# Green's 60 comparators for blocks of 16 rows, in place of the odd-even merges' 63, in the sort of a quantile kernel

## The chip, the core and the metric

The kernel runs on one core of a Trainium2 chip. Its engines are TensorE (PE, matmuls), VectorE (DVE, elementwise), ScalarE (ACT, here mostly copies), GpSimd (POOL, here the issuer of indirect DMAs) and SyncE (SP, plain DMAs). They run side by side and wait for each other by semaphores. The metric is device time in microseconds, the median of several runs.

## What is computed

Two graph layers over 4096 nodes of 128 features. The first is an attention layer with 8 heads over the neighbours that the 4096 x 4096 matrix `adj` names. The second takes, for every node and every feature, three quantiles of the neighbours' values; only it matters here:

```python
keep = mask & ~remove                  # each node's neighbours, some removed
n_keep = keep.sum(axis=1)
vals = jnp.where(keep[:, :, None], x[None, :, :], big)
svals = jnp.sort(vals, axis=1)
for q in (0.25, 0.5, 0.75):
    idx = jnp.maximum(jnp.ceil(q * n_keep).astype(jnp.int32) - 1, 0)
    picked = jnp.take_along_axis(svals, idx[:, None, None], axis=1)[:, 0, :]
    agg = agg + w_q * picked
```

The mean of the three is mixed half and half with the node's own value, goes through a 128 x 128 linear layer, and `x` is added.

## The kernel before

The first part (lines 160 to 1430) finds the neighbours of every node and computes the attention layer; it fills roughly the first 4000 us. A branch on a flag then chooses between `general`, a dense path that isn't taken with these inputs, and `sparse` (line 1699), the sort.

**Tiles.** `sparse` works through 32 tiles of 128 nodes, one node in each partition. The nodes are ordered by their number of neighbours, so that tile t needs at most `HIGH[t]` rows: 50 for tile 0, rising to 80 for tile 30 and 100 for tile 31. `load` (line 1884) gathers a tile's rows with one indirect DMA of POOL for each row (line 1726): a row is one neighbour's 128 float32 features in every partition, 128x128 elements. The tile `rows` has three buffers, and tile t+1 is loaded ahead of the phase of tile t. Missing neighbours are filled with very large and very small values.

**The network.** The rows are put in order by a sorting network: fixed pairs (a, b) of rows, of which the smaller goes to a and the larger to b, for all nodes and features at once. `swap_layers(w)` (line 1501) gives the pairs for w rows in layers: Batcher's odd-even merges, with n the power of two from w upwards. `comparators(n)` (line 1441) yields the pairs of numbers (p, k) with p = 1, 2, 4, ..., n/2, and for each p, k = p, p/2, ..., 1. The layers with p below 16 sort each block of 16 rows, in 10 layers and 63 comparators; those with p = 16 and p = 32 merge the blocks. `needed_swaps` (line 1513) drops the comparators, or single outputs of one, that no wanted rank depends on. A tile with 66 to 80 rows sorts 64 of them in this way and the others apart (`plan`, line 1682), and `quantile` (line 1779) joins the two lists for the ranks that may be picked.

**Steps.** `steps` (line 1578) makes instructions of a layer's comparators: those with the same distance b - a whose lower rows form a regular pattern (runs in a grid of up to two strides, `rectangles`, line 1540) are one step, cut (`pieces`, line 1561) to at most `PAIRS` = 16 comparators. `compare` (line 1751) emits a step. Where both outputs are needed, ACT copies the lower rows aside (line 1764), and DVE takes the minimum of copy and upper rows into the lower rows and the maximum into the upper ones (line 1771). The copy is in one of two PSUM buffers named `low` if it has more than `SMALL` = 4 rows, else in one of four buffers named `low_s`. Steps with one needed output are one DVE instruction without a copy (lines 1775 and 1777).

**Order.** `plan` cuts a tile's layers in two: `second` is the last merge (6 layers for 64 rows), `first` all before it. In phase t, `interleave` (line 1612) mixes `second` of tile t-1 and `first` of tile t: from the steps whose predecessors are done it always takes the one that DVE can begin soonest by a small count of costs. Behind the list, `quantile` and `pick` of tile t-1 are added; the pieces of `pick` and `finish` (ACT's scaling of the picked rows at line 1826, PE's sums at 1833 and 1861, ACT's copies at 1843 and 1869) stand in the list `waiting` and are emitted one at a time between later steps, the PE pieces only beside a step of 5 to 12 rows. The framework that assigns semaphores may still move single instructions a little, such as a maximum behind the next step's minimum.

Of the kernel before, what the change touches and what calls it, by code (L numbers as in the profile page):

```python
# [1440 lines left out]
def comparators(n):  # L1441

    p = 1
    while p < n:
        k = p
        while k:
            yield p, k
            k //= 2
        p *= 2
# [48 lines left out]
    return a  # L1498


def swap_layers(w):

    n = 1 << (w - 1).bit_length()
    for p, k in comparators(n):
        yield [
            (i + j, i + j + k)
            for j in range(k % p, n - k, 2 * k)
            for i in range(k)
            if (i + j) // (2 * p) == (i + j + k) // (2 * p) and i + j + k < w
        ]  # L1510
# [171 lines left out]
def plan(t):  # L1682

    wide = HIGH[t]
    extra = wide - MAIN if MAIN < wide <= 80 else 0
    w = wide - extra
    needed = {i - 1 for lo, hi in places(t) for i in range(lo - extra, hi + 1)}
    layers = needed_swaps(swap_layers(w), needed)
    merge = (w - 1).bit_length()

    first = steps(layers[:-merge], lambda i: i, PAIRS if t else PAIRS // 4)
    second = steps(layers[-merge:], lambda i: i)
    if extra:
        apart = needed_swaps(swap_layers(extra), range(extra))
        first += steps(apart, lambda i: MAIN + extra - 1 - i)
    return first, second, extra
# [650 lines left out]
```

## Time and profile before

| | |
|---|---|
| median of 3 timed runs | 8359.05 us (8342.91 to 8362.36) |
| span of the profiled execution | 8384.6 us |
| attention layer and neighbour search | to about 4000 us |
| quantile sort | from about 4000 us to the end |
| two-output comparisons on DVE (line 1771) | 2768 instructions, 4044.6 us busy |
| copies for them on ACT (line 1764) | 1384 instructions, 1708.2 us busy |
| gathers of rows on POOL (line 1726) | 2078 instructions, 2031.9 us busy |

The profile is of one execution, taken by the hardware profiler. Its span runs from the first to the last instruction. A page gives busy time and idle time by engine, and groups of instructions by source line, with the shapes of output and inputs; "128x2048" is 128 partitions by 16 rows of 128 features. "idle before" is time in which the engine stood still just ahead of the group, with what released it. A timeline gives start, length, engine, line and operation, in microseconds.

### The profile page before, as it was taken

What the parts mean: (1) busy time and instruction counts of PE and PEld (TensorE: products, weight loads), DVE (VectorE), ACT (ScalarE), POOL (GpSimd) and SP (SyncE); (2) the same over time, 40 slices, a digit from 0 to 9 for tenths busy, and PEclk for the clock granted to TensorE, in tenths of its full rate; (3) what the DMA queues carried; (4) which work ended last, traced back from release to release, by engine and by line L of the source; (5) the groups of instructions that cost most, each with busy time, mean ns of one, the idle gap of its engine ahead of it and who ended that gap; (6) DMA issues with size and microseconds to landing.
All of it is one profiled execution on the core that took longest, in us unless ns stands there. A gap on an engine that the chain in (4) does not pass through costs nothing. (4 is left out here: it accounts for less than half of the span.)

```text
span 8384.6 us, 31455 instructions
## 1 busy us (share of the span) xinstructions
PE 1235.7 (15%) x6047; PEld 1032.2 (12%) x6047; DVE 5886.7 (70%) x9454; ACT 2218.9 (26%) x2338; POOL 4358.1 (52%) x4524
## 2 busy tenths in 40 slices
PE   2122222222332332330000000000000000000000
PEld 1121212222231322230000000000000000000000
DVE  6454564454222222224899999999999999999899
ACT  5021121000000000002344443443443433333333
POOL 3545546656666666666455456445554545354410
PEclk5565656565565666565555555555555555555555
DMA  6122222112112111111011111111111111011100
GB/s 192 43 89 71 74 77 64 49 38 50 50 48 50 50 49 50 50 41 39 26 36 35 33 36 43 31 32 38 34 34 31 38 30 35 27 34 32 31 9 1
DMA packets 219060, 380.98 MB, mean 45 GB/s; under 512 B 129283, under 2 KB 129412, under 8 KB 218852
## 3 DMA queue, kind: packets, MB, share of 16 engines
q0 software_dynamic: 145808, 308.58, 13.9%
q1 hardware_dynamic: 72898, 70.23, 2.8%
q14 instruction: 159, 1.30, 0.1%
q8 instruction: 49, 0.80, 0.0%
q10 hardware_dynamic: 146, 0.07, 0.0%
HBM read 368.26 MB, written 10.31 MB: 45 GB/s over the span
## 5 line engine op out<-in xcount | busy, mean ns | idle before, releaser
L1771 DVE TENSOR_TENSOR rows<-low,rows 128x2048 f32<-128x2048 f32 (+10 forms) x1970 | 3649.3, 1893 | 88.0 <-ACT low L1764 61.7
L1726 POOL DMA_INDIRECT rows<-x_d,info x2078 | 2031.9, 978 | 1863.7 <-ACT picked L1826 1184.2
L975 POOL DMA_INDIRECT nb<-xf_d,ids x2190 | 2078.1, 949 | 1329.5 <-issue 625.3
L1764 ACT COPY low<-rows 128x2048 f32<-128x2048 f32 (+8 forms) x985 | 1528.4, 1557 | 2331.8 <-DVE rows L1771 1665.3
L1115 PE MATMUL ps_z<-spread,nb 128*128 128x128 f32 x4500 | 757.9, 325 | 1491.4 <-issue 737.3
L1107 DVE TENSOR_TENSOR spread<-e,ps_small 128x1152 f32<-128x1152 f32 (+4 forms) x312 | 342.2, 1109 | 804.1 <-remote 594.0
L1115 PEld LDWEIGHTS ps_z<-spread,nb 128*128 128x128 f32 x4500 | 702.4, 237 | 1565.9 <-issue 996.7
L1833 PE MATMUL low<-sixth_i,picked 128*128 128x128 f32 x300 | 74.3, 430 | 4347.7 <-ACT low L1764 3413.6
L1833 PEld LDWEIGHTS low<-sixth_i,picked 128*128 128x128 f32 x300 | 65.0, 322 | 4357.0 <-ACT low L1764 3420.9
L1771 DVE TENSOR_TENSOR rows<-low_s,rows 128x512 f32<-128x512 f32 (+3 forms) x798 | 395.3, 523 | 128.7 <-remote 39.9
L1077 ACT ACTIVATE ps_e<-e 128x256 f32<-128x256 f32 (+4 forms) x64 | 26.1, 408 | 1513.9 <-DVE e L1067 556.2
L190 DVE MAX8 k<-key 128x8 f32<-128x256 f32 x416 | 169.0, 416 | 169.6 <-remote 119.5
L1764 ACT COPY low_s<-rows 128x512 f32<-128x512 f32 (+3 forms) x399 | 179.8, 486 | 281.6 <-DVE rows L1771 172.0
L1873 POOL DMA_INDIRECT out<-o,info x32 | 34.9, 1091 | 397.2 <-ACT o L1869 369.3
L1130 ACT COPY zT<-ps_z 128x512 f32<-128x512 f32 x64 | 37.6, 587 | 742.7 <-remote 586.0
L382 ACT ACTIVATE nz<-a_i 128x1024 bf16<-128x1024 int32 x128 | 134.2, 1049 | 328.9 <-remote 198.6
L190 DVE MAX8 lists<-cand 128x8 f32<-128x176 f32 x416 | 128.1, 332 | 69.7 <-remote 47.1
L192 DVE MATCH_REPLACE8 key<-k,key 128x256 f32<-128x256 f32 x384 | 156.1, 408 | 0.0
L1058 DVE TENSOR_TENSOR e<-nb,ps_small 128x64 f32<-128x64 f32 (+9 forms) x200 | 45.2, 237 | 154.4 <-DMA nb<-xf_d,ids 129.9
L1438 DVE SCALAR_TENSOR_TENSOR zT<-zT,ps_h 128x512 f32<-128x512 f32 x64 | 42.0, 682 | 158.0 <-ACT zT L1437 109.7
L1146 PE MATMUL ps_h<-zT,w_ga 128*128 128x256 f32 x256 | 105.3, 569 | 271.3 <-DVE s L1438 157.2
L1775 DVE TENSOR_TENSOR rows<-rows 128x256 f32<-128x256 f32 (+8 forms) x245 | 142.5, 583 | 1.6 <-DVE rows L1771 1.4
(245 smaller groups left out, 2429.0 us busy)
## 6 DMA issues: line engine op xcount, KB each, us to landing
a_i<-in_adj SPq DMA_DIRECT2D x128, 512.0 KB
nb<-xf_d,ids POOLq DMA_INDIRECT x2190
rows<-x_d,info POOLq DMA_INDIRECT x2078
xf_d<-xf POOLq DMA_DIRECT2D x4, 576.0 KB
xf<-in_x POOLq DMA_DIRECT2D x4, 512.0 KB
meta_d<-rowdata_k SPq DMA_DIRECT2D x4, 324.0 KB
abc_ta<-in_L_gnn_a POOLq DMA_DIRECT2D x2, 512.0 KB
w_ga<-in_L_gnn_W POOLq DMA_DIRECT2D x2, 512.0 KB
```

What stands on the lines that cost most here:

```text
L190: nc.vector.max(out=top, in_=work)
L192: nc.vector.match_replace(out=work, in_to_replace=top, in_values=work, imm_value=gone)
L382: nc.scalar.activation(nz[:, j, :], a_i, AF.Relu, scale=-1.0, accum_out=self.negative[:, k : k + 1],)
L975: gather = nc.gpsimd.indirect_dma_start(out=rows[:, used + i, :], out_offset=None, in_=xf_d, in_offset=bass.IndirectOffsetOnAxis(ap=ids[:, ...
L1107: last = nc.vector.tensor_tensor(spread[:, :m], e[:, at : at + m, :].unsqueeze(2).to_broadcast(shape), own.unsqueeze(1).unsqueeze(3).to_br ...
L1115: product = nc.tensor.matmul(ps_z[:, g, :], rows[:, k, :D], spread[:, i].rearrange("p j h -> p (j h)"), start=i0 + i == 0, stop=i0 + i == ...
L1146: nc.tensor.matmul(ps_h[:, k, :], w_sb[:, h0 + k, :], zT[:, h0 + k, :], start=True, stop=True)
L1726: return nc.gpsimd.indirect_dma_start(out=row, out_offset=None, in_=x1_d, in_offset=bass.IndirectOffsetOnAxis(ap=info[:, col : col + 1], a ...
L1764: nc.scalar.copy(packed, lows)
L1771: done = nc.vector.tensor_tensor(to, packed, highs, op=op)
L1775: nc.vector.tensor_tensor(lows, lows, highs, op=ALU.min)
L1833: product = nc.tensor.matmul(made["ps"], v, to, start=i == 0, stop=i == len(found))
```

## The change

The layers with p below 16 are replaced by a fixed list of ten layers, `SIXTEEN`, applied to every block of 16 rows. Its first four layers compare rows at distances 1, 2, 4 and 8; six irregular layers with 28 comparators follow, so that a block has 60 comparators in place of 63, in as many layers. It is used where the number of rows is 0 or 14 modulo 16 (16, 62, 64 here); at other widths, and for the merges with p = 16 and 32, nothing is changed. In a block cut short by w, comparators that reach beyond w are left out.

```diff
+SIXTEEN = [[(i, i + k) for i in range(16) if not i & k] for k in (1, 2, 4, 8)] + [
+    [(1, 2), (3, 12), (4, 8), (5, 10), (6, 9), (7, 11), (13, 14)],
+    [(1, 4), (2, 8), (7, 13), (11, 14)],
+    [(2, 4), (3, 8), (5, 6), (7, 12), (9, 10), (11, 13)],
+    [(3, 5), (6, 8), (7, 9), (10, 12)],
+    [(3, 4), (5, 6), (7, 8), (9, 10), (11, 12)],
+    [(6, 7), (8, 9)],
+]
+
+
 def swap_layers(w):
 
     n = 1 << (w - 1).bit_length()
+    whole = w % 16 in (0, 14)
+    for layer in SIXTEEN if whole else []:
+        yield [(i + a, i + b) for i in range(0, n, 16) for a, b in layer if i + b < w]
     for p, k in comparators(n):
+        if whole and p < 16:
+            continue
         yield [
             (i + j, i + j + k)
             for j in range(k % p, n - k, 2 * k)
```

## The prediction

> **What bounds the kernel now.** I read the page's busy times and its forty slices first, then the windows of the sorting stage, then the groups by form, then what VectorE waited for, and last single instructions in the timeline.
>
> ```profile
> PE 1235.7 (15%) x6047; PEld 1032.2 (12%) x6047; DVE 5886.7 (70%) x9454; ACT 2218.9 (26%) x2338; POOL 4358.1 (52%) x4524
> ...
> DVE  6454564454222222224899999999999999999899
> ACT  5021121000000000002344443443443433333333
> POOL 3545546656666666666455456445554545354410
> ```
>
> The 70% of DVE is an average over two halves. From slice 20 on, which is from about 4000 us, its digit is 8 or 9 and nobody else's is above 6. That half is the quantile sort, the only code the change reaches. The windows of that half give the share more exactly (columns: window, its length, then busy us and number of instructions of PE, PEld, DVE, ACT, POOL):
>
> ```profile
> 5500.00:6000.00 500.00, 17.87 (x64) 14.60 (x64) 493.00 (x308) 200.22 (x151) 266.32 (x267) 0.50 0.12 35
> 6000.00:6500.00 500.00, 17.45 (x62) 14.18 (x62) 492.31 (x350) 201.18 (x163) 244.15 (x249) 0.50 0.12 33
> 6500.00:7000.00 500.00, 17.45 (x62) 14.18 (x62) 495.82 (x439) 200.97 (x190) 258.72 (x258) 0.50 0.12 34
> ```
>
> DVE works 98.5 to 99.2% of these windows, ACT 40%, POOL about 51%. So a microsecond of DVE work taken out here is a microsecond of the span, as long as DVE stays that full. What it waits for between 5300 and 8000 us, in the table of waits (total us, times, longest):
>
> ```profile
> DVE rows L1771 <- ACT low L1764: 50.0, 18, 22.5
> DVE rows L1771 <- issue: 5.2, 10, 1.6
> ```
>
> Of the 50.0 us, 22.5 and another 14.1 are two single waits (at 7773 and 7127 us) in which the ACT copy in question stood behind the copy of an output from PSUM (L1869), itself late. The other 16 are 13.4 us together, some 0.8 us each.
>
> **The price of one comparison step.** A step with both outputs is an ACT copy of the k lower rows (L1764) and a minimum and a maximum on DVE (L1771), each over 128k elements. From the groups by form (mean ns is the figure before the second bar) and the timeline of DVE:
>
> ```profile
> L1771 DVE TENSOR_TENSOR rows<-low,rows 128x2048 f32<-128x2048 f32 x910 | 2052.7, 2282 | 20.9 <-ACT low L1764 12.0 <-issue 3.2 <-DVE rows L1771 0.5
> L1764 ACT COPY low<-rows 128x2048 f32<-128x2048 f32 x455 | 848.8, 1869 | 1256.0 <-DVE rows L1771 900.6 <-issue 343.4 <-DMA rows<-x_d,info 8.3
> L1771 DVE TENSOR_TENSOR rows<-low,rows 128x1024 f32<-128x1024 f32 x334 | 405.3, 1219 | 30.8 <-ACT low L1764 22.5 <-issue 1.6 <-DVE rows L1771 0.8
> ...
> L1764 ACT COPY low<-rows 128x1024 f32<-128x1024 f32 x167 | 169.6, 1016 | 366.7 <-DVE rows L1771 220.9 <-issue 144.0 <-DVE rows L1777 1.7
> ```
>
> ```profile
> 6118.35 2.28 DVE L1771 TENSOR_TENSOR rows<-low,rows 128x2048 f32<-128x2048 f32 x1
> 6120.54 0.68 DVE L1771 TENSOR_TENSOR rows<-low_s,rows 128x512 f32<-128x512 f32 x1
> 6121.14 1.22 DVE L1771 TENSOR_TENSOR rows<-low,rows 128x1024 f32<-128x1024 f32 x1
> 6122.28 0.68 DVE L1771 TENSOR_TENSOR rows<-low_s,rows 128x512 f32<-128x512 f32 x1
> 6122.88 1.22 DVE L1771 TENSOR_TENSOR rows<-low,rows 128x1024 f32<-128x1024 f32 x1
> ```
>
> The recorded lengths overlap. After the 2048 the next starts 2.19 us later, not 2.28; after the 512, 0.60 (not 0.68); after the 1024, 1.14 (not 1.22). A 512 and a 2048 differ by 1.60 us for 1536 elements, 1.042 ns each, so an instruction takes **0.067 us plus 0.133 us for each row** of 128 elements from start to start.
>
> **The sum.** The plan of each tile can be counted from the code before and after. Widths that are 0 or 14 modulo 16 occur in 20 of the 32 tiles; the merge of the last six layers (`second`) is the same in all.
> - 16 tiles sort 64 rows (HIGH 64 to 76): 5 more steps, so 10 more DVE instructions, and 12 fewer comparators (3 in each of 4 blocks), so 24 fewer row operations: 0.67 - 3.20 = -2.53 us each, -40.5.
> - 3 tiles of 62 rows: 14 more instructions, 22 fewer row operations: -1.99 us each, -6.0.
> - tile 30 (64 rows and 16 apart): 24 more, 30 fewer: -2.4.
>
> Together 226 more instructions (+15.1) and 480 fewer row operations (-64.0): **-48.9 us** of DVE. What changes is the mix: of the steps with both outputs, 111 with 16 rows go and 154 with 8 rows come, 42 with 4, 20 with 12 and some small ones; 1112 steps become 1225. ACT gets 113 copies more, but shorter ones: -111 x 1.87 + 154 x 1.02 and the rest come to -6 us, on an engine that is idle 60% of the stage.
>
> Here a rule speaks against the change. The Trainium skill's "VectorE: DVE Perf Modes" gives a fp32 tensor_tensor (N+151)/0.96 ns (section on the TRN2 errata; it advises tiles of 512 elements and more) and says that the next instruction does not start until the pipeline is empty (section "The DRAIN you can't avoid"). Its length agrees with the rows: (512+151)/0.96 = 691 ns against 684. But as the price of an instruction it would be 0.157 us for each of the 226, +35.5, and leave only -28.5. The starts above say 0.067. The rows of this trace decide; the rule's sum is kept as a rival.
>
> **Dependent neighbours.** Where an instruction needs what the one straight ahead of it on DVE did, the overlap is lost:
>
> ```profile
> 6009.70 6.88 DVE L1771 TENSOR_TENSOR rows<-low,rows 128x2048 f32<-128x2048 f32 x3
> ```
>
> Three free 2048s would take 2.20 + 2.20 + 2.28 = 6.68; here the third takes rows that the second wrote, and 0.20 is lost. A maximum straight behind its own minimum loses 0.13 in the same way (starts 6014.29 and 6016.61 against 2.20). In the order in which the built programs issue on DVE, neighbours of the first kind fall from 128 to 88 and of the second from 165 to 137, because layers of four blocks have two to five steps that are independent of each other, which the greedy list can lay between. 40 x 0.2 + 28 x 0.13 = **-11 us**. From both sides: none of it (the waits only move elsewhere) or all of it; I take all, since it is the issue order itself that is counted.
>
> **Waits for the copy.** A new layer such as (1,4),(2,8),(7,13),(11,14) is two steps of 8 rows, and the next layer's copies need both. A copy of 8 rows is 1.02 us, and the other step's pair beside it is 2 x 1.13, so one independent step covers it; where there is none, the merge steps of the tile before lie between. Bounds: all 16 short waits go (-13), or each of the 20 changed phases gets one more of 1.60, such as the one at 5623.99 us (+32). The copy is nearer to covered (ACT idles 60%), so I take 0.
>
> **What else it touches.** All other instructions are the same and in the same order outside this stage; POOL's gathers are as many (2078 rows). Three row buffers let tile t+1 be gathered during phase t: a gather is issued every 1.25 us, so 66 rows need 83 us of a phase of 124 to 164 us, and a phase shorter by 2.5 us is still covered. The exception is tile 31, with 100 rows: its gathers run from 7875.3 to 8002.4 us, and DVE waits for them at the end of tile 30's phase (2.7 us at 8002). So tile 30's 2.4 us are lost there: +2.4. After that only tile 31 is left (100 rows, unchanged), and its chain ends the program.
>
> Sum: -48.9 - 11 + 2.4 = -57.5. It is made in an execution of span 8384.6; the median of the three timed runs is 8359.05, 25.5 below, while the two long waits above are 36.6 of that span. The sum is of work and does not hang on them. Carried to the median: 8359 - 57.5 = **8301.5 us**, 0.7% faster.
>
> **The rivals.**
> - **Copies come late (slower).** Every added step leaves DVE waiting for its copy. For it: the steps get smaller, and chains of dependent layers are where the waits of today lie. Price: a whole 8-row copy bare, 1.02 us, on 113 steps is +115: 8417. It decides from 0.51 us an added step (57.5 / 113), and is a measurable loss from 0.73. Against: ACT at 40%, two jobs interleaved, and fewer dependent neighbours in the issue order.
> - **The full length counts.** If DVE empties its pipe behind each added instruction, the sum is -28.5 + 2.4: 8333, just at the edge. Against: the starts shown.
> - **Nothing reaches the end.** Gathers or the release of row buffers set the pace of a phase, as for tile 31, and the saved DVE time turns into waiting: 8359. For it: POOL waits 1184 us for row buffers in the page's groups (L1726 behind L1826), so buffers are the limit of gathering. Against: this waiting is POOL's slack; DVE's waits for rows are the one at 8002 us and the first tiles'.
> - **The network isn't one that sorts, or the widths don't occur.** Counted from the plans above, 20 tiles change; a later half of the blocks cut at 62 keeps only comparators below 62, and the rows missing are the largest. I give it nothing.
>
> **Numbers.** As summed 0.76, copies late 0.07, full length 0.09, nothing reaches the end 0.08. A change within 0.3% (25 us) can't be told from none here: the three runs before differ by 19 us. Below: -57.5 - 13 and a run low by 10 gives 8278. Above: the full length's 8333 with a run high by 6: 8339. Range 8276 to 8339. Faster takes the first case and most of the second, 0.84; same 0.10; slower 0.06, the late copies.
>
> **What would show it.** In the profile after: the 128x2048 group of L1771's successor falls by 222, the 128x1024 group grows by 308; DVE's instructions grow by 226, and its busy time, in which overlaps count once (2052.7 / 910 = 2.256), falls by about 50 us. DVE's total wait for ACT copies between 5300 and 8000 should stay near 13 us beside any single long wait. Wrong would be: starts behind 8-row instructions more than 1.14 us apart without a wait (the pipe price), or a wait for ACT at each new layer.

## The result, and the profile after

| | kernel before | changed kernel |
|---|---|---|
| median, 9 runs each, in one session | 8349.96 us (8342.91 to 8362.47) | 8375.19 us (8366.08 to 8382.18) |
| span of the profiled execution | 8384.6 us | 8373.4 us |

The ratio is 1.0025, with a 95% interval of 1.0017 to 1.0034. The changed kernel is slower by 25 us; 58 us less were forecast. (The two profiled spans have the opposite order: that execution of the kernel before was a long one, and entered the sort at 3825.6 us. A second profile of it entered at 3792.5 us, with a span of 8350.8. So the sort is compared below by its own length. In the changed kernel it is longer by 15 to 16 us; the rest of the 25 us lies ahead of it, in code that is the same in both and took 3792.5 to 3825.6 us in three profiled executions.)

The work did shrink as counted. From the page of the changed kernel, busy time by engine and the slices of DVE and ACT:

```profile
PE 1241.1 (15%) x6047; PEld 1038.0 (12%) x6047; DVE 5839.2 (70%) x9680; ACT 2213.3 (26%) x2451; POOL 4353.9 (52%) x4524
...
DVE  6554565463222222224899999999999998997999
ACT  5021121000000000002344444444433343342433
```

DVE has 226 more instructions and is busy 47.5 us less (5886.7 before); ACT has 113 more and is busy 5.6 us less. The groups by form, mean ns of one ahead of the second bar:

```profile
L1786 DVE TENSOR_TENSOR rows<-low,rows 128x2048 f32<-128x2048 f32 x688 | 1546.1, 2280 | 62.8 <-ACT low L1779 51.7 <-issue 8.3
L1786 DVE TENSOR_TENSOR rows<-low,rows 128x1024 f32<-128x1024 f32 x642 | 761.2, 1216 | 36.9 <-issue 29.8 <-ACT low L1779 3.2
```

222 of the 16-row instructions went and 308 of 8 rows came. What did not stay is DVE's share. The same windows as before and two later ones (window, length, busy us and instructions of PE, PEld, DVE, ACT, POOL):

```profile
5500.00:6000.00 500.00, 17.86 (x64) 14.60 (x64) 497.92 (x360) 206.42 (x176) 256.07 (x264) 0.50 0.13 35
6000.00:6500.00 500.00, 17.45 (x62) 14.18 (x62) 479.59 (x381) 198.19 (x178) 267.02 (x277) 0.50 0.14 36
6500.00:7000.00 500.00, 7.08 (x28) 6.19 (x28) 495.95 (x486) 200.74 (x208) 217.11 (x226) 0.50 0.11 30
7000.00:7500.00 500.00, 15.36 (x54) 12.39 (x54) 466.96 (x457) 189.42 (x195) 246.27 (x247) 0.50 0.12 32
7500.00:8000.00 500.00, 15.79 (x56) 12.82 (x56) 428.03 (x398) 175.19 (x181) 224.82 (x233) 0.50 0.13 31
```

Of the kernel before, the prediction showed the first three of these windows, with 98.5 to 99.2%. The other two were less full already (96.8 and 94.2%), and there stand its two long waits:

```profile
7000.00:7500.00 500.00, 15.37 (x54) 12.40 (x54) 484.15 (x436) 194.00 (x181) 223.46 (x227) 0.50 0.11 30
7500.00:8000.00 500.00, 15.80 (x56) 12.82 (x56) 470.96 (x383) 191.57 (x173) 249.54 (x259) 0.50 0.13 34
```

In the changed kernel DVE is full between the stalls (99.6% in the first window), but three windows lack 20 to 72 us each. DVE's waits between 5300 and 8000 us, which were 50.0 us and at most 22.5 before:

```profile
DVE rows L1786 <- ACT low L1779: 74.1, 10, 48.6
DVE rows L1786 <- issue: 44.1, 12, 29.6
DVE rows L1786 <- remote: 9.8, 4, 3.1
```

Every gap of the sort can be added up from the starts of DVE's instructions: from one start to the next, less 0.066 us and 1.042 ns for each element. That price comes from the starts that the prediction showed; a gap is what is left over.

| us | before | changed | difference |
|---|---|---|---|
| instructions at that price | 4279.1 | 4230.0 | -49.1 |
| gaps under 0.1 us | 5.3 | 8.6 | +3.3 |
| gaps of 0.1 to 0.3 us (dependent neighbours) | 44.3 | 33.9 | -10.4 |
| gaps of 0.3 to 3 us | 139.1 | 136.5 | -2.6 |
| gaps over 3 us | 72.3 (9) | 146.2 (14) | +73.9 |
| sort, first to last start | 4539.2 | 4554.3 | +15.1 |

So the gain is there, and a few long waits took more than it brought. The longest, in the timelines of PE, ACT and DVE of the changed kernel (start, length, engine, line, operation; in brackets the idle time before and its releaser):

```profile
7692.71 0.80 PE L1876 MATMUL low<-xs,idf 128*128 128x128 f32 x2 [15.73 <-ACT low L1779]
...
7699.78 0.80 PE L1876 MATMUL low<-lwT,comT 128*128 128x128 f32 x2
```
```profile
7693.41 1.87 ACT L1779 COPY low<-rows 128x2048 f32<-128x2048 f32 x1 [0.76 <-issue]
7747.39 0.58 ACT L1884 COPY o<-low 128x512 f32<-128x512 f32 x1 [52.11 <-remote]
7748.01 3.67 ACT L1779 COPY low<-rows 128x2048 f32<-128x2048 f32 x2
```
```profile
7686.70 14.66 DVE L1786 TENSOR_TENSOR rows<-low,rows 128x2048 f32<-128x2048 f32 x7
7749.91 6.69 DVE L1786 TENSOR_TENSOR rows<-low,rows 128x2048 f32<-128x2048 f32 x3 [48.55 <-ACT low L1779]
```

At the end of each group of four tiles PE does the linear layer: 12 matmuls, 24 passes in the trace (two each), recorded as over by 7700.6. The copy of their result (L1884) starts only at 7747.39. The comparison copy behind it in ACT's queue waits with it, and DVE waits for that one. In the kernel before, ACT at the same place:

```profile
7766.48 0.61 ACT L1764 COPY low_s<-rows 128x512 f32<-128x512 f32 x1
7793.66 0.58 ACT L1869 COPY o<-low 128x512 f32<-128x512 f32 x1 [26.56 <-remote]
```

The page names DVE's wait after the comparison copy and ACT's as "remote", a releaser that it does not resolve; it is found by the semaphore events: the semaphore that PE raises after a matmul moves at 7704.0, 7726.4, 7737.6 and last at 7747.37, 0.02 us before the copy. At the end of group 1, where no row gather runs, it moves 0.01 us after the last matmul (4546.54 and 4546.53). Here 37 row gathers were issued between 7692 and 7739, one each 1.25 us.

So the wait was there before too, 26.6 us of ACT and 22.5 of DVE here and 14.1 at one more group end, and 22.5 and 13.9 in the second profile: it is no accident of one execution. What the change moved is when the matmuls come. The pieces in `waiting` are taken one for each two-output step, and PE's only beside steps of 5 to 12 rows. By the plans, the list `first` of a 64-row tile has 35 such steps instead of 30, and 15 instead of 6 of 8 to 12 rows; the whole phase of the longest wait has 61 instead of 56, and 23 instead of 14 of 5 to 12 rows. So `waiting` is worked off sooner: in that phase the last sums' copy comes 44 us after the first row gather was issued (7682.3 against 7638.3), and 82 us before the change (7763.4 against 7681.4). The gathers take 100 us in both. The matmuls that stood near their end now stand in their middle. How late the copy came after the last matmul, at the ends of groups 5, 6 and 7: 1.3, 14.6, 21.0 us before; 15.9, 27.7, 46.8 after. In all six cases the copy starts 9 to 13 us after the phase's last row gather was issued (10.0, 10.0 and 13.1 us before; 9.7, 11.2 and 9.3 after): what comes late in these phases is released shortly behind the end of the gathers.

### The profile page after: what moved, and what is told of

Same layout as the page of the kernel before. It is cut to its first block, busy times and chain, and to the rows that moved or that the text cites. A ratio compares the mean times of both kernels' runs of the same rounds, so it can differ in the third digit from the quotient of the medians.

```text
span 8373.4 us, 31685 instructions
## 1 busy us (share of the span) xinstructions
PE 1241.1 (15%) x6047; PEld 1038.0 (12%) x6047; DVE 5839.2 (70%) x9680; ACT 2213.3 (26%) x2451; POOL 4353.9 (52%) x4524
## 5 line engine op out<-in xcount | busy, mean ns | idle before, releaser
L1786 DVE TENSOR_TENSOR rows<-low,rows 128x1024 f32<-128x1024 f32 (+8 forms) x2076 | 3527.5, 1745 | 139.5 <-ACT low L1779 84.7
L1779 ACT COPY low<-rows 128x2048 f32<-128x2048 f32 (+9 forms) x1038 | 1488.8, 1440 | 2141.8 <-DVE rows L1786 1619.5
L1786 DVE TENSOR_TENSOR rows<-low_s,rows 128x512 f32<-128x512 f32 (+3 forms) x918 | 462.2, 534 | 143.2 <-remote 45.3
L1779 ACT COPY low_s<-rows 128x512 f32<-128x512 f32 (+3 forms) x459 | 211.4, 496 | 402.2 <-DVE rows L1786 254.8
L1130 ACT COPY zT<-ps_z 128x512 f32<-128x512 f32 x64 | 37.6, 588 | 775.1 <-remote 628.0
```

The costliest lines, as they stand in the source:

```text
L1779: nc.scalar.copy(packed, lows)
L1786: done = nc.vector.tensor_tensor(to, packed, highs, op=op)
```

## The experiments

The theory after the first look: PE's output matmuls complete late while row gathers run, and that hides the network's gain. Rivals: the network's shorter steps cost more by themselves; or those matmuls are slow whatever runs. The runs are from four chips. On three of them the kernel before takes 8350 to 8382 us; the fourth, called the faster chip below, is another case, to which a paragraph of its own comes back. Unless said otherwise a ratio is against the kernel before on the same chip, with its 95% interval. "Late" is the copy's start after the recorded end of the last matmul, at groups 5, 6, 7.

**Moving the matmuls in time.** First a second look at the kernel before (8352.57 us), then three kernels in which only the moment of the output changes.

> The kernel before, unchanged, for a profile of an ordinary execution: the profile at hand spans 8384.6 us, 35 us over the median of the timed runs. If the two long waits in it (14.1 and 22.5 us, behind output sums of TensorE that completed late) come and go from run to run, this one shows less of them: span near 8348 with long waits of 0 to 25 us. If they are always there, the span is near 8385 again and the median was something else.

Eighteen empty entries in the list ahead of the output, in the changed kernel:

```diff
-            return [("bank", layer), ("copy", layer_copy)]
+            return [*[("copy", lambda: None)] * 18, ("bank", layer), ("copy", layer_copy)]
```

> The changed kernel, but the four output sums of a group of tiles are issued 18 steps (about 45 us) later, when the row gathers of that phase are over. Theory A (the gain of the network, some 57 us, is there, but the sums now fall into the middle of the gathers, TensorE's completions come 16 to 47 us late there, the copy of their result stands in ACT's queue ahead of the comparison copies, and DVE waits): the four long waits, some 95 us, go, and the time falls from 8375 to 8280-8305. Theory B (the shorter steps themselves cost more than the rows say): nothing of the network changes here, so the time stays within 10 us of 8375.

8448.33 us, 1.0114 (1.0099 to 1.013). Eight such entries in the kernel before:

> The kernel before with the output sums 8 steps (about 26 us) later, which takes them past the end of the gathers there. Theory A: what long waits it ordinarily has (0 to 37 us) go: 8315 to 8350. Theory B: unchanged, 8350.

8511.83 us, 1.0185 (1.0171 to 1.0199). Both forecasts failed, and in the same way. (Group 7, for which they were meant, did come sooner, 8.8 and 12.5 us late.) The entries that were meant to carry the late groups past the gathers carried the early ones into the next phase's. Groups 1 to 5 of the first are now 8 to 34 us late and groups 1 to 4 of the second 30 to 33, where groups 1 to 4 had been on time in both (0.04 us); groups 5 and 6 of the second came on time. Then the other way, the output earlier in the kernel before, its network untouched:

```diff
-APART = 22
+APART = 12
```

> The kernel before, its network untouched, with the sums of the picked rows 12 steps behind their scaling instead of 22, so that they and the output sums fall some 33 us earlier, into the middle of the gathers, as in the changed kernel. Theory A: it gets the changed kernel's long waits, 40 to 90 us: 8385 to 8440. Theory B: unchanged within 10 us of 8350.

8516.38 us, 1.0197 (1.0181 to 1.0212). The copies are 36.1, 50.2 and 56.6 us late, with waits of DVE of 37.4, 52.6 and 60.0, the last two in the sums of this line of its waits between 5300 and 8000 us:

```profile
DVE rows L1771 <- ACT low L1764: 139.7, 22, 60.0
```

The old network with matmuls amid the gathers loses far more than the new one lost, so the new network's shorter steps aren't needed for such a loss.

**No gathers in flight.** Of the row gathers that run beside the output of groups 5 to 7, all but the first are put behind the output's scatters on POOL:

```diff
+                if t in (22, 26, 30) and s >= 24:
+                    behind.append((rows[:, s, :], info, s))
+                else:
+                    gather(rows[:, s, :], info, s)
...
+                with tc.issue_after(last.ins):
+                    for row in behind:
+                        gather(*row)
```

> The changed kernel, with the order on GpSimd's queue altered at three places only: of the row gathers of tiles 22, 26 and 30, the first 24 are issued as before, and the others stand behind the output's scatters of the group that ends in that phase. So no row gather is in flight while TensorE does the twelve output matmuls of groups 5, 6 and 7. The sort's steps, the copies and the products are the same. Theory A (TensorE's completions come late while row gathers are in flight, the output copy waits for them in ScalarE's queue and VectorE behind it): the three output copies come within 3 us of the last matmul instead of 15.9, 27.7 and 46.8 us, the waits of 16.8, 29.7 and 48.6 us on VectorE go, and the kernel takes 8275 to 8305 us, faster than both. Theory B (these matmuls are slow at that place by themselves): no change, 8365 to 8385 us. Theory C (the gathers are what sets the end, and moving them back makes rows late): over 8385 us, with waits of VectorE for DMA.

> The kernel before, with the same edit, the first 40 gathers issued as before since its output products come some 80 us into the phase. Theory A: the output copies of groups 6 and 7 are on time, the waits of 14 and 22.5 us go, 8313 to 8335 us; and the changed kernel with this edit is faster than this one by 45 to 60 us, which is what the network itself is worth. Theory B: no change, 8340 to 8362 us. If the network is worth nothing, both kernels with the edit take the same time.

8399.67 us, 1.0026 (1.0016 to 1.0036), and 8423.89 us, 1.0064 (1.0048 to 1.0081). All six copies came 0.04 us after the last matmul, from up to 46.8. At group 3 of the first, where rows were not held, the copy was 6.4 us late beside 10 gathers in the same execution. So the completions are late only beside gathers. But the time did not fall, because the held rows came late and DVE waited for them instead, 38.5, 21.9 and 29.6 us in the first. Two more, on the faster chip, with as many rows ahead as those traces seemed to allow (44, 40, 28; and 48, 50 for tiles 26 and 30 of the kernel before):

> The changed kernel with the gathers held back as in e5_after_gate, but with 44, 40 and 28 of the rows of tiles 22, 26 and 30 issued at once, so that by the times of that run the rest has landed before the next tile's first step needs it. Theory A: the copies are on time (0 to 2 us), no wait for rows takes their place, ratio 0.991 to 0.9935 against the kernel before (some 85 us less than the changed kernel). If the waits are moved to the rows whatever is done: 0.999 to 1.003.

> The kernel before with 48 and 50 rows of tiles 26 and 30 issued at once and the rest behind the scatters (tile 22 is left alone, its copy was 1.3 us late). Theory A: the waits of 14 and 22.5 us go, ratio 0.9955 to 0.997; and the distance to e10_after_gate2 is what the network is worth once the output copy is on time, 40 to 60 us.

0.9974 (0.9964 to 0.9984) and 1.003 (1.0018 to 1.0041); medians 7506.12 and 7547.51. DVE's waits:

```profile
DVE rows L1786 <- ACT low L1779: 40.6, 13, 25.9
DVE rows L1786 <- ACT low_s L1779: 9.6, 1, 9.6
```
```profile
DVE rows L1771 <- ACT low L1764: 41.5, 18, 25.9
```

The 26 us are the rows of tile 30 in both: neither forecast was met. The medians differ by 41.4 us in favour of the new network, though its gaps over 3 us, here most of them waits for rows, are 11 us more (66.2 and 55.3). All copies of groups 1 to 7 are on time, but on this chip that shows nothing of the held rows:

**The faster chip.** It ran these two, the kernel before in four pieces and the first kernel with 6 matmuls below, and takes 7524.71 us for the kernel before. There next to nothing comes late. In the trace of the kernel before with held rows, 652 of the 654 matmuls that raise a semaphore have its move within 0.1 us of their recorded end, in the attention layer beside its gathers too (on a usual chip 323 of 654, where part of the moves is missing from the trace). It enters the sort at 3097 us, not 3800, and DVE's gaps of 0.3 to 3 us are 29 to 40 us in the sort, not some 140. The wait of the attention layer's costliest DVE group beside its gathers, in the kernel before on a usual chip and in the one with held rows on this chip:

```profile
L1107 DVE TENSOR_TENSOR spread<-e,ps_small 128x1152 f32<-128x1152 f32 (+4 forms) x312 | 342.2, 1109 | 804.1 <-remote 594.0
L1107 DVE TENSOR_TENSOR spread<-e,ps_small 128x1152 f32<-128x1152 f32 (+4 forms) x312 | 342.7, 1109 | 185.0 <-PE ps_z L1115 138.3
```

So its runs can't show what a remedy does against late completions. They are compared with each other alone, and the changed kernel without an edit did not run there.

**Fewer or shorter bursts of matmuls.** Without the product of ones and bias, 8 matmuls a group:

```diff
-                        (c["ones"][0:1, :], b_row[:, j, :]),
```

> The changed kernel without the product of the ones and the bias row (a matmul over one partition) in the output, so 8 matmuls a group, not 12; the bias is left out of the output. Theory A1 (each matmul over one partition is what stalls while gathers run): the output copies come on time, 8275 to 8310 us. Theory A2 (a burst of TensorE instructions stalls beyond some length, whatever they are; the sums' 10 passes come 1 to 2 us late beside gathers and 12 passes 5 us): the waits shrink by about a third to a half, 8325 to 8350 us. Theory A3 (TensorE's completions are held until the gathers end): no change, 8365 to 8385 us.

8359.99 us, 0.9974 (0.9965 to 0.9984). Late: 20.0, 18.5, 30.2. So that product is not the cause; with fewer matmuls groups 6 and 7 came sooner, group 5 did not. In four pieces of 3 matmuls, each with a copy of its own:

```diff
-            return [("bank", layer), ("copy", layer_copy)]
+            return [
+                (kind, lambda *ps, part=part, j=j: part(*ps, j))
+                for j in range(m)
+                for kind, part in (("bank", layer), ("copy", layer_copy))
+            ]
```

> The changed kernel with the output of a group done in four pieces of 3 matmuls (6 passes), each with a copy of its own, one piece beside a comparison step after the other, and no piece of 12 matmuls. The arithmetic is the same. Theory A1 (each output matmul of one kind costs some 11 us beside gathers): each of the four copies is about 11 us late, 8370 to 8420 us. Theory A2 (only a burst of more than about 10 passes stalls): all copies come within 3 us, the long waits go, 8280 to 8315 us. Theory A3 (completions are held until the gathers end): the first copy of a group is as late as the whole was, no change, 8365 to 8390 us.

> The kernel before with the output in four pieces of 3 matmuls, as in e8_after_split. Theory A2: its two long waits shrink below 10 us in sum, ratio 0.996 to 0.9985, and the distance to e8_after_split (0.9949) is 10 to 30 us or more, in favour of the changed network. If the network is worth nothing by itself, this kernel is as fast as e8_after_split.

The changed kernel: 8329.49 us, 0.9949 (0.9933 to 0.9964), faster than both kernels. Most pieces are 1 to 6 us late, the latest of groups 5 to 7 11 to 14. The kernel before, on the faster chip, got slower: 1.0103 (1.0088 to 1.0119). There the scaling of picked rows, which frees a row buffer, comes late in the list that now holds eight entries for a group, not two (4932.2 us); the gathers of tile 16 start behind it at 4933.8, 170 us after those of tile 15 (134 in the kernel before with held rows on the same chip), and DVE waits 34.6 us for its rows. So this pair says nothing of the networks.

**As many columns, half as many matmuls.** The products with the identity and with ones are one matmul over four tiles' 512 columns each, 6 matmuls (12 passes) in place of 12; the values stay:

```diff
+                terms = [
+                    (0, m, c["idf"], xs[:, :m, :]),
+                    (0, m, c["ones"][0:1, :], b_row[:, :m, :]),
+                ] + [(j, 1, comT[:, j, :], wT) for j in range(m)]
```

> The changed kernel with the output of a group done by 6 matmuls, not 12: the products of the identity and of the ones with four tiles are one matmul over 512 columns each, the four with the weights stay. As many columns go through TensorE, the values are the same. Theory A2 (beside gathers each TensorE instruction beyond the first few takes some 2.8 us a pass, by the 5.6 us steps between the semaphore updates in the runs so far): 12 passes instead of 24, so the copies of groups 5 to 7 are at most 5, 10 and 20 us late instead of 15.9, 27.7 and 46.8, and the time falls by 45 to 65 us against the changed kernel: ratio 0.9945 to 0.997 against the kernel before. If the delay goes by columns: as late as before, ratio 1.001 to 1.004. Theory A3 (completions are held until the gathers end): no change either.

0.9911 (0.9898 to 0.9925) on the faster chip, 7458.59 us, with every copy 0.04 us late. By the paragraph above that is no merit of the 6 matmuls; it does show that where nothing comes late the new network with this edit is 66.1 us faster than the kernel before. Then on one chip of the usual kind (kernel before 8381.90 us) the changed kernel, both kernels with this edit, and one with six short products of ones and bias put back, 12 matmuls again:

```diff
+                    *[(0, 1, c["ones"][0:1, :], b_row[:, 0, :])] * 6,
```

> The changed kernel as it is, for comparison on the same chip as the next three. Ratio 1.001 to 1.004 against the kernel before, as first measured; the output copies of groups 5 to 7 late by 10 to 50 us.

> The kernel before with 6 output matmuls of a group in place of 12. Theory A2: the copies of groups 6 and 7 are on time, the waits of 14 and 22.5 us go, ratio 0.995 to 0.997.

> The changed kernel with 6 output matmuls, as e9_after_wide, on the chip of the other three. Ratio 0.988 to 0.993; 75 to 100 us less than e13_after_again (the waits of 16.8, 29.7, 4.6 and 48.6 us in the profile of the changed kernel), and 40 to 65 us less than e14_before_wide, which is what the network is worth when no copy is late (the sum said 57.5).

> e9_after_wide with six more matmuls of the ones with the bias row into the first tile's columns, so that 12 matmuls (24 passes) stand in the group as in the changed kernel; the bias row is added seven times to one tile of each group. Theory A2 (the number of TensorE's instructions decides): the copies of groups 5 to 7 are late again by 10 to 40 us, 30 us or more slower than e15_after_wide_again. If the kind of matmul decides (the identity's and the weights' 128 columns at a time): on time, at most 10 us slower than e15_after_wide_again.

| kernel | passes | late (groups 5, 6, 7) | median us | ratio |
|---|---|---|---|---|
| changed | 24 | 16.2, 30.6, 46.1 | 8411.22 | 1.0038 (1.0023 to 1.0052) |
| before, 6 matmuls | 12 | 8.6, 17.6, 21.3 | 8380.97 | 0.9996 (0.9988 to 1.0005) |
| changed, 6 matmuls | 12 | 13.7, 6.4, 16.4 | 8339.63 | 0.9945 (0.9928 to 0.9962) |
| changed, 6 and 6 short ones | 24 | 21.0, 29.7, 46.1 | 8422.80 | 1.005 (1.0035 to 1.0065) |

PE's and ACT's timelines of the third at the end of group 7, then ACT's of the fourth:

```profile
7691.35 2.07 PE L1875 MATMUL low<-xs,idf 128*128 128x512 f32 x2 [15.95 <-issue]
7693.36 2.07 PE L1875 MATMUL low<-lb,ones 1*128 1x512 f32 x2
7695.36 2.08 PE L1875 MATMUL low<-lwT,comT 128*128 128x128 f32 x8
```
```profile
7692.06 1.87 ACT L1779 COPY low<-rows 128x2048 f32<-128x2048 f32 x1 [0.76 <-issue]
7713.84 0.59 ACT L1883 COPY o<-low 128x512 f32<-128x512 f32 x1 [19.92 <-issue]
```
```profile
7736.65 1.87 ACT L1779 COPY low<-rows 128x2048 f32<-128x2048 f32 x1 [0.76 <-issue]
7790.63 0.58 ACT L1884 COPY o<-low 128x512 f32<-128x512 f32 x1 [52.12 <-remote]
```

With half the matmuls ACT stands 19.9 us where it stood 51 to 52, and the changed kernel gains 71.6 us; with six more it loses all of it, and is as late as at first (46.1). The number of matmuls decides there, not their columns; that the six put back are short ones of one row speaks against the kind. Half the matmuls get through amid the gathers: the copy at group 7 of the third starts 22.5 us after the first matmul, while gathers are still issued. In the kernel before, 12 passes gain nothing: its copies are as late as with 24, against the expectation. The traces suggest why. At group 7 its matmuls begin at 7767.4, the last gather ends at 7785.4, and the copy starts at 7794.8. The 12 passes of the changed kernel took 12.5 and 22.5 us amid gathers at groups 6 and 7. Here the gathers go on for some 18 us, so that the copy is released behind the gathers' end, as with 24 passes. No run was made to test this.

The 6-matmul edit and the split one make the changed kernel faster than both kernels of the comparison, by 0.55% and 0.51% against the kernel before.

## Why the prediction was wrong

- **The price and the sum of work held.** (Its range should have begun at 8278 by its own sum, not 8276; nothing hangs on that.) -48.9 forecast, -49.1 by the starts; busy time down by 47.5 where about 50 was named. The rule of the full length would have shown as longer gaps; those under 0.1 us grew by 3.3 in all, not by 20. That rival is out. It had read half of its source: in the Trainium skill's "VectorE: DVE Perf Modes", the section "The DRAIN you can't avoid" adds that a next instruction which is not held starts earlier, as the starts here do (0.60 us after a 512 whose length is 0.68).
- **Dependent neighbours held:** -11 forecast, -10.4.
- **ACT's copies for the comparisons** were taken as 0 and are nearly so: gaps of 0.3 to 3 us changed by -2.6, with one place against it, below.
- **Tile 30 was mis-sized.** Its 2.4 us were to be lost to tile 31's gathers. DVE's gaps over 0.3 us near the end of its phase and in its quantiles are 18.9 us in the changed kernel and 7.7 in the kernel before, +11.2 (with 6 matmuls 18.2 and 7.7). The waits stand between small steps, most of them of 2 rows, and their copies. DVE there in the changed kernel, then at the same place with 6 matmuls on the faster chip:

```profile
7977.86 0.43 DVE L1786 TENSOR_TENSOR rows<-low_s,rows 128x256 f32<-128x256 f32 x1 [3.10 <-remote]
7979.26 0.43 DVE L1786 TENSOR_TENSOR rows<-low_s,rows 128x256 f32<-128x256 f32 x1 [0.97 <-issue]
...
7985.56 0.43 DVE L1786 TENSOR_TENSOR rows<-low_s,rows 128x256 f32<-128x256 f32 x1 [3.98 <-issue]
7986.96 1.36 DVE L1786 TENSOR_TENSOR rows<-low_s,rows 128x256 f32<-128x256 f32 x3 [0.97 <-DVE rows L1786]
```
```profile
7066.05 2.77 DVE L1786 TENSOR_TENSOR rows<-low_s,rows 128x256 f32<-128x256 f32 x8
7068.73 0.42 DVE L1792 TENSOR_TENSOR rows<-rows 128x256 f32<-128x256 f32 x1
7069.07 2.37 DVE L1786 TENSOR_TENSOR rows<-low_s,rows 128x256 f32<-128x256 f32 x6
```

  From 7958.3 to 7995.9 us these are 39 instructions in 37.6 us with 18.3 us of gaps over 0.3; on the faster chip the same 39 take 19.2 us without one. So small steps are not slow by themselves; on the usual chips they wait long for their copies beside gathers, and the change put more of them there.
- **The step that failed** is "The sum is of work and does not hang on them", said of the two long waits behind the output copy, with the 0 for waits beside it. Those waits are a term of the sum, put at nothing: gaps over 3 us grew by 73.9, more than the 57.5 forecast. The prediction moved steps of the sort and left the list `waiting`, which is counted in those steps, where it was. "All other instructions are the same and in the same order outside this stage" was true, and the output matmuls are inside it.
- **The rivals.** The slower one was right in the engine and wrong in the place: not 113 comparison copies late by half a microsecond each, but three output copies late by 16 to 47. "Nothing reaches the end" falls too: with 6 matmuls in both kernels the network is worth 41.3 us (8380.97 less 8339.63; copies are still late in both), with held rows on the faster chip 41.4.
- **What is missing to 57.5** with 6 matmuls, from the same kind of sum for those two kernels (43.8 over the sort): instructions -49.1, dependent neighbours -10.6, gaps under 0.1 us +3.3, of 0.3 to 3 us +6.5, over 3 us +6.2. Tile 30's +10.5 is most of the last two.

Shown by runs on the usual chips: that the copies are late only beside gathers (six group ends with held rows in two kernels, all 0.04 us), that halving the matmuls takes away some 72 us of waits in the changed kernel and putting six back restores them, and that the network gains 41 with the same edit in both kernels. That the network's extra steps bring the output forward is read from the plans and the trace; moving the output by hand in the kernel before cost in the same way. On the faster chip next to no completion is late; whether the changed kernel as it is would have met its forecast there was not run.

## What to carry to other kernels

Work that is hung on the steps of a loop moves when the number of steps changes, even if nobody touched it: list what is issued "one for each step", and see what it runs beside before and after. A long wait that returns at the same place in a second profile belongs in the sum, however few there are. On another chip of the same kind the same kernel may not have these waits at all, so a result of this sort is compared on one chip. In an in-order queue one late copy stops all behind it, so what feeds it should be short, or stand where nothing delays it.

## What the runs showed of the hardware

On three of four chips TensorE's completions come late while GpSimd issues indirect gathers one each 1.25 us; on the fourth they don't. In the longest cases the semaphore's recorded moves come 22.4, 11.2 and 9.8 us apart in the changed kernel, over 4, 2 and 2 matmuls, so about 5 to 5.6 us for each, and 5.6 us apart at two group ends of the kernel with 18 empty entries. The copy came up to 56.6 us late. In the recorded passes a matmul takes 0.66; the recorded matmul ends show nothing of the delay. Short bursts get through: in the later phases the sums' 10 passes beside gathers were at most 4 us late, 12 passes 5 to 6. Where the gathers end first, the copy mostly follows 8 to 16 us after the last one was issued. With 18 empty entries 24 passes twice got through amid the gathers, in 34 and 42 us. It isn't uniform: the changed kernel's group 3 was on time in one execution beside 7 gathers and 7.4 us late in another.

What holds the matmuls up is open. A transfer of instructions it was not in the longest case: none is on record between 7639.1 and 7748.6 us, and the copy started at 7747.39. One rival stands untested, that the recording of the execution has a part in it. On the three usual chips the traces lack many records, on the faster one hardly any: of the 8043 moves of DVE's semaphore 5823 are there in the kernel before, and 8044 in the one with held rows on the faster chip; of the landings of DMAs some 15700 and 75900. A recorder that falls behind and engines that come late may have one cause, or one may bring the other; no run here tells.
